# Storing the fp8 copy of an adjacency chunk one chunk later in the written order (20 slots behind its load instead of 10)

## The chip, the cores and the metric

The kernel runs on one core of a Trainium2 chip. A core has four engines that compute, each with its own queue of instructions: TensorE (PE, matrix products), VectorE (DVE), ScalarE (ACT) and GpSimd (POOL). A fifth, SyncE (SP), issues DMAs. DMAs are issued here from the queues of SyncE, of GpSimd and, at the start, of ScalarE. The metric is the time of one execution on the device in microseconds (us); of several runs the median is taken.

## The reference, cut to what matters

Sixteen graphs of 1024 nodes with 128 features go through four layers, each `x = layernorm(x + layer(x, adj))`. `adj` is a 0/1 matrix in float32, one for each graph.

```
layer 0: masked attention: softmax over the neighbours of relu(q) relu(k)^T, times relu(v)
layer 1: h[n] = max over m of relu(x[n] (W1 - W2) + x[m] W2 + b) * adj[n, m]
layer 2: MLP((1 + eps) x + adj^T x), masked by node
layer 3: adj_d = dilate(adj)            # a row-by-row removal of edges, each row seeing earlier removals
         three rounds of batchnorm(relu(sage(h, adj_d))), then a linear layer of the three results
```

Two parts of this set the kernel's shape. Layer 1 is a maximum over neighbours, not a product, and the removal of edges in layer 3 is serial over the 1024 rows. The removal depends on the adjacency alone, so it can run beside layers 0 to 2.

## The kernel before, in words

Layers 0 to 2 and the removal of edges share one long stage, the function `layers_012`; layer 3 follows.

**The slots.** Layer 1 takes 12 neighbours at a time (`PS`, L44). For each such group a table over the subsets of its two halves of six is built, and each node looks up the best neighbour in its subset by matrix products. A graph has 86 groups (`NP`, L47), and one group of one graph is a *slot*: 16 x 86 = 1376 slots, in the loop at L932, each written out by `slot` (L861). In a slot, PE multiplies the transposed adjacency by a table of signs (`count`, L812) to find the subset of every node, ACT turns the result into a one-hot matrix (L813), PE looks up (L843), and DVE takes the maximum (L908). Between these steps a planner in the kernel (`advance`, `dilate_on`) puts in the other layers' work and the removal.

**The chunks.** The transposed adjacency arrives in chunks of 120 rows (`CH`, ten groups of 12), nine for a graph, the ninth of 64 rows. `load_columns(at)` (L753) does two things for chunk number `at`, counted through all graphs, 0 to 143. It writes the *store* of chunk `at - 1` (L758), a DMA on SyncE's queue that copies the fp8 chunk from the buffer AT to the DRAM tensor `adj8`, which layer 3 reads in place of the float32 original (`load_near`, L993). Then it writes the *load* of chunk `at` (L764), a DMA on GpSimd's queue that reads float32 and writes fp8 into AT. AT has four buffers (L761), so the load of chunk `at` writes where chunk `at - 4` was, and needs that one's store and its matrix products to be done. The first two calls are at L916; then `slot` calls it at every tenth group (L873), two chunks ahead of the one in use.

**What sets the order.** Inside the block at L930, PE, ACT, DVE and POOL take their instructions in the order in which the kernel writes them. SyncE isn't among them: the order of its DMAs is made by the scheduler that builds the program. Each queue works from the front, so a DMA that waits for its input holds those behind it.

**What shares SyncE's queue.** The removal of edges goes over blocks of 32 rows. Per block it has `above` and V (L555, L556), the exchange of `hit` through DRAM (L686, L689), the results `removed` from the buffer `gone` (L615, two buffers, made at L613), `removed_T` (L622), and its reading back into `gone_T` (L517). Beside these are the loads of X (L747) and the stores of the layers' results (L466). After the slots come `near` (L995) and the weights of layer 3 (L118).

The store and the load, as written before:

```
nc.sync.dma_start(out=adj8[before][k * CH:k * CH + rows], in_=AT[at - 1][:rows])
...
nc.gpsimd.dma_start(out=t[:rows], in_=adjT[b, c * CH:c * CH + rows])
```

Of the kernel before, what the change touches and what calls it, by code (L numbers as in the profile page):

```python
# [39 lines left out]
B, N, D, H2 = 16, 1024, 128, 256  # L40
P = 128
T = N // P
GS = 6
PS = 2 * GS  # L44
PC = 10
CH = PC * PS
# [28 lines left out]
def tile_graph_layers(ctx: ExitStack, tc, a, out):  # L75
    nc = tc.nc
# [95 lines left out]
    for b in range(B):  # L172
        q, g = divmod(b, G)
        nc.gpsimd.dma_start(out=half_rows[g * R:(g + 1) * R, :, q],
                            in_=a["nodemask"][b].rearrange("(k r) -> r k", r=R))
# [21 lines left out]
    adj8 = [dram.tile([N, N], F8, name=f"adj8_{b}") for b in range(B)]  # L197
# [44 lines left out]
    def layers_012():  # L242
# [133 lines left out]
        def attend(b):  # L376
            for t in range(T):
                yield ask("PE", 0.01, after=("e", b, t))
                if t == 0:
                    y = w4.tile([P, T, D], F32, name="y0", tag="xT")  # L380
                e, total = exps.pop((b, t))
                eT = w4.tile([P, T, P], F32, name="eT")
                for h in range(2):
                    yield ask("PE", 0.44, take=True, same=(h == 0))
                    p = shared("pe")
                    for c in range(4):
                        nc.tensor.transpose(p[:, c * P:(c + 1) * P],  # L387
                                            e[:, (4 * h + c) * P:(4 * h + c + 1) * P], ident)
                    yield ask("A", 0.59, give=True, same=True)
                    nc.scalar.copy(eT[:, 4 * h:4 * h + 4, :].rearrange("p c i -> p (c i)"), p)  # L390
                happened["back", b, t] = now
                for h in range(4):
                    yield ask("PE", 0.45, take=(h == 0), same=(h > 0))
                    if h == 0:
                        pav = shared("pav")[:, :D]
                    for c in range(2 * h, 2 * h + 2):
                        nc.tensor.matmul(pav, eT[:, c, :], values[b][:, c, :], start=(c == 0), stop=(c == T - 1))  # L397
                yield ask("V", 0.4, give=True)
                share = small.tile([P, 1], F32, name="share")
                nc.vector.reciprocal(share, total)  # L400
                nc.vector.scalar_tensor_tensor(y[:, t, :], pav, share, X[b][:, t, :], op0=ALU.mult, op1=ALU.add)
            yield from norm(X[b], y)
            happened["X1", b] = now
# [66 lines left out]
        def tables_of(b):  # L470

            if b:
                yield ask("V", 0, urgent=True, after=("tables", b - 1))
            for g0 in range(0, NP, TG):
                n_g = 2 * min(TG, NP - g0)
                yield ask("V", 0.01, same=True, urgent=True, after=("q", b))
                made.append((b, g0))
                yield ask("V", 0.1, same=True, urgent=True, after=("used", *made[-3]) if len(made) > 2 else None)
                qg = qs[b].rearrange("o (g s) -> o g s", s=GS)
                subs[b, g0] = w2.tile([P, TG, P], F32, name="sub", bufs=2)  # L480
                sub = subs[b, g0].rearrange("o t (a s) -> o (t a) s", a=2)
                nc.vector.memset(sub[:, :n_g, 0:1], LOWEST)
                for k in range(GS):
                    n = 1 << k
                    yield ask("V", 0.06 + n * n_g / 960, same=(n < 8), urgent=True)
                    nc.vector.tensor_max(sub[:, :n_g, n:2 * n], sub[:, :n_g, 0:n],  # L486
                                         qg[:, 2 * g0:2 * g0 + n_g, k:k + 1].to_broadcast([P, n_g, n]))
                happened["sub", b, g0] = now
            happened["tables", b] = now
# [255 lines left out]
        def load_x(b):  # L745
            X[b] = apool.tile([P, T, D], F32, name="X", bufs=3)
            nc.sync.dma_start(out=X[b], in_=x[b].rearrange("(t p) d -> p t d", p=P))  # L747
# [4 lines left out]

        def load_columns(at):  # L753
            b, c = divmod(at, T + 1)
            if at:
                before, k = divmod(at - 1, T + 1)
                rows = min(CH, N - k * CH)
                nc.sync.dma_start(out=adj8[before][k * CH:k * CH + rows], in_=AT[at - 1][:rows])  # L758
            if b < B:
                rows = min(CH, N - c * CH)  # L760
                t = AT[at] = apool.tile([CH, N], F8, name="AT", bufs=4)  # L761
                if rows < CH:
                    nc.gpsimd.memset(t, 0.0)
                nc.gpsimd.dma_start(out=t[:rows], in_=adjT[b, c * CH:c * CH + rows])  # L764

        An, AT, subs, qs, ps, values, exps, bests, hots, tables = ({} for _ in range(10))
# [8 lines left out]
        def start(stream, first=False):  # L775
            pending[stream] = [next(stream, None), -9]
            streams.insert(0 if first else len(streams), stream)
# [52 lines left out]
        def low_part(s):  # L830
            pt, high = tables[s]
            nc.tensor.matmul(pt, less, high, start=False, stop=True, skip_group_check=True)  # L832
            low = w2.tile([P, 2 * P], F32R, name="low", bufs=2)
            nc.scalar.copy(low, pt)  # L834
            tables[s] = high, low

        def look_up(s, h, pg):

            at = s % 2
            for k, part in enumerate(tables[s - at]):  # L840
                for a in range(2):
                    rows = slice(64 * a, 64 * a + 64)
                    nc.tensor.matmul(pg[:, a], part[rows, at * P:(at + 1) * P], hots[s][rows, halves[h]],  # L843
                                     start=(k == 0), stop=(k == 1))
# [9 lines left out]
        def dilate_on():  # L854
            nonlocal due, wants_bank
            if due <= now and not (wants_bank and taken >= 2 and given.get(taken - 2, 1e9) > now):
                after, cost, wants_bank = next(dilate, (B * NP, 0, False))
                due += after
                room["V"] -= cost

        def slot(s, last):  # L861

            nonlocal now
            now = s
            b, g = divmod(s, NP)
            if s >= 0 and g == 0:
                bests[b] = bests[b - 1] if b else w4.tile([P, 2, N], F32, name="best")
                if b + 1 < B:
                    start(tables_of(b + 1), True)
                    load_x(b + 1)  # L870
                    start(attend(b + 1))
                    start(scores(b + 1))
            if s >= 0 and g % PC == 0 and b * (T + 1) + g // PC + 2 <= B * (T + 1):  # L873
                load_columns(b * (T + 1) + g // PC + 2)
            for h in range(2):
                now = s + 0.5 * h
                for e in ROOM:
                    room[e] = min(room[e] + ROOM[e] / 2, ROOM[e] / (2 if e in ("PE", "V") else 1))
                if s >= 0:
                    pg = psum.tile([P, 2, 512], F32, tag="wide", name="pg", bufs=2)  # L880
                    look_up(s, h, pg)
                early = s >= 0 and due < now
                if early:
                    dilate_on()
                advance(("PE",))
                advance(("A", "V", "Pool"))
                if s >= 0 and not early:
                    dilate_on()
                if h == 0 and s % 2 and s + 1 < last:
                    low_part(s + 1)  # L890
                if s + 2 < last:
                    count(s + 2, h)
                    if h and s % 2 == 0:
                        table(s + 2)
                if s >= 0:
                    own = bests[b][:, :, halves[h]]
                    if g == 0:
                        if b:
                            if h:
                                merge(b - 1, h)  # L900
                            total(b - 1, h)
                        nc.vector.tensor_copy(own, pg)
                        if b and h:
                            start(rest(b - 1))
                    else:
                        if g == NP - 1 and h:
                            merge(b, 0)
                        nc.vector.tensor_max(own, own, pg)  # L908
            if s >= 0:
                hots.pop(s)  # L910
# [19 lines left out]
        with tc.manual_schedule(engines={mybir.EngineType.PE, mybir.EngineType.Activation, mybir.EngineType.DVE,  # L930
                                         mybir.EngineType.Pool}):
            for s in range(-2, B * NP):  # L932
                slot(s, B * NP)
# [437 lines left out]
```

## Time and profile before

| what | value |
|---|---|
| median of three runs | 6206.11 us |
| the three runs | 6195.82, 6206.11, 6211.7 us |
| the profiled execution | 6199.75 us, span 6198.0 us |
| granted TensorE clock, mean | 0.962 |
| stage of the slots | about 90 to 5085 us of the span |
| layer 3 after it | 5085 to 6198 us |
| chunk stores at L758 | 144, on SyncE's queue, first at 28.2 us, last at 5023.5 us |
| chunk loads at L764 | 144, on GpSimd's queue, first at 19.8 us, last at 5020.3 us |
| a load from issue to landing | 2.9 us least, 3.9 median, 29.7 most |

The *span* runs from the first to the last instruction of the profiled execution. *Busy* is the time in which an engine computes; issuing a DMA isn't counted as busy, so SyncE has no busy time, and what it does is read from its waits and its timeline. In a view of waits, a row has the engine that waited and the line of the instruction, then what it waited for, then the total in us, the number of waits and the longest one. SPq is SyncE's queue. In a timeline, a row has the start in us, the duration, the engine, the line and the operation; rows of the same kind that follow each other are merged, with their number at the end (x2), and the duration then runs from the first start to the last end. What stands in brackets is idle time of the engine before the instruction and what ended it. *Landing* is the moment at which a DMA's data have arrived.

### The profile page before, as it was taken

Reading aid. Unit: us, or ns where it says so; the run is one execution under the profiler, and the core shown is the slowest. Engines: PE = TensorE matmul, PEld = TensorE weight load, DVE = VectorE, ACT = ScalarE, POOL = GpSimd, SP = SyncE. Lnnn points to the kernel's source line nnn. Section 1 sums busy time; section 2 is a strip of 40 time slices with the busy share of each in tenths; the row PEclk is TensorE's granted clock in tenths of the full one; section 3 lists DMA queues with packets and bytes.
Section 4 is the critical chain, followed back from the end, with each engine's and each line's share of the span. In section 5 each row is a group of like instructions: output and inputs, shape, how many; then the busy total and the mean of one; then the engine's idle time right before and its main releaser. Section 6 shows DMA issues by size and latency. Waiting matters only on the chain.

```text
span 6198.0 us, 93287 instructions
## 1 busy us (share of the span) xinstructions
PE 5582.7 (90%) x30144; PEld 3046.0 (49%) x30250; DVE 4870.0 (79%) x7484; ACT 3988.2 (64%) x7362; POOL 3613.1 (58%) x11879
## 2 busy tenths in 40 slices
PE   5989899989898989999989798989999878999998
PEld 4545454545454545454545454545444435555654
DVE  3888788888888888889888788888889875555455
ACT  3767676767676767677767576767666554344855
POOL 2676666667666767677777757667677651110114
PEclk8999999989999999999999899999999989999999
DMA  5021213121212212122121211212121014554645
GB/s 42 11 33 25 40 22 42 22 40 24 40 24 31 32 32 32 32 32 38 26 43 22 39 24 31 31 31 33 31 33 28 19 41 124 159 144 133 214 163 191
DMA packets 496976, 334.28 MB, mean 54 GB/s; under 512 B 303338, under 2 KB 448228, under 8 KB 492388
## 3 DMA queue, kind: packets, MB, share of 16 engines
q1 hardware_dynamic: 405504, 260.29, 14.5%
q0 software_dynamic: 89008, 67.42, 12.6%
q8 instruction: 237, 3.88, 0.3%
q14 instruction: 255, 2.09, 0.1%
q10 hardware_dynamic: 1972, 0.59, 0.1%
HBM read 362.38 MB, written 133.96 MB: 80 GB/s over the span
## 4 chain that ended last, share of the span: by engine, by line
PE 31%; DVE 10%; ACT 4%; POOL 3%; issue 2%; DMA 1%; SPq 0%; DVEq 0%; POOLq 0%; ACTq 0%
PE pg L843 7%; PE pagg L1071 5%; DVE best L908 5%; PE pm L812 3%; PE po L1101 2%; PE po L1095 1%; PE pa L439 1%; PE pav L397 1%; PE pp L300 1%; ACT hot L813 1%; PE pdeg L1026 1%; DVE near L1014 1%; PE psc L349 1%; PE prank L599 1%; PE pe L387 1%
## 5 line engine op out<-in xcount | busy, mean ns | idle before, releaser
L908 DVE TENSOR_TENSOR best<-best,pg 128x1024 f32<-128x1024 f32 x2720 | 3259.3, 1214 | 512.6 <-PE pg L843 501.7
L813 ACT ACTIVATE hot<-pm,one_less 128x512 fp32r<-128x512 f32 x2752 | 1887.4, 689 | 780.5 <-PE pm L812 773.2
L843 PE MATMUL pg<-hot,high 64*128 64x512 f32 x5504 | 1407.3, 508 | 258.9 <-DVE best L908 220.8
L843 PE MATMUL pg<-hot,low 64*128 64x512 f32 x5504 | 1115.5, 402 | 0.0
L812 PE MATMUL pm<-AT,lit 120*128 120x512 fp8e4 x2752 | 1085.9, 395 | 4.5 <-ACT low L834 3.5
L843 PEld LDWEIGHTS pg<-hot,high 64*128 64x128 f32 x5504 | 523.5, 187 | 1014.6 <-DVE best L908 492.8
L669 POOL TENSOR_SCALAR sc<-low_counts,half_mask,rest 16x1 f32<-16x1 f32 x992 | 354.4, 357 | 393.9 <-DVE rest L655 283.2
L843 PEld LDWEIGHTS pg<-hot,low 64*128 64x128 f32 x5504 | 537.9, 192 | 0.0
L812 PEld LDWEIGHTS <-lit 120*128 120x128 fp8e4 x2752 | 270.3, 98 | 389.8 <-issue 313.5
L674 POOL TENSOR_SCALAR sc<-sc 16x1 f32<-16x1 f32 x992 | 393.1, 396 | 105.1
L834 ACT CAST low<-pt 128x256 fp32r<-128x256 f32 x688 | 256.0, 372 | 263.3 <-PE pt L832 261.9
L671 POOL TENSOR_SCALAR sc<-sc 16x1 f32<-16x1 f32 x992 | 324.5, 327 | 107.6
L1116 POOL TENSOR_TENSOR length<-length,mhalf 128x8 f32<-128x8 f32 x48 | 78.9, 1644 | 489.2 <-DVE length L1115 489.2
L676 POOL TENSOR_SCALAR hit<-V,sc 16x31 bf16<-16x31 bf16 (+30 forms) x992 | 362.4, 365 | 0.0
L677 POOL TENSOR_SCALAR last_rank<-V,sc 16x31 f32<-16x31 bf16 (+30 forms) x992 | 342.9, 346 | 0.0
L832 PE MATMUL pt<-high,less 128*128 128x256 f32 x688 | 279.2, 406 | 67.6 <-ACT high L827 61.5
L824 PE MATMUL pt<-ident,sub 128*128 128x128 f32 x1376 | 277.5, 283 | 51.8 <-ACT hot L813 50.0
L486 DVE TENSOR_TENSOR sub<-sub,q 128x24 f32<-128x24 f32 (+11 forms) x768 | 304.0, 397 | 24.8 <-ACT q L304 10.4
L397 PE MATMUL pav<-v,eT 128*128 128x128 f32 x2048 | 301.5, 292 | 2.0 <-ACT eT L390 2.0
L397 PEld LDWEIGHTS pav<-v,eT 128*128 128x128 f32 x2048 | 255.4, 196 | 73.3 <-issue 55.7
L670 POOL TENSOR_SCALAR sc<-sc 16x1 f32<-16x1 f32 x992 | 237.0, 239 | 86.5
L349 PE MATMUL psc<-kT,qT 128*128 128x256 f32 x1024 | 276.3, 388 | 9.9 <-issue 9.9
(270 smaller groups left out, 9662.9 us busy)
## 6 DMA issues: line engine op xcount, KB each, us to landing
removed<-gone SPq DMA_DIRECT2D x128, 256.0 KB
An<-in_adj_dram POOLq DMA_DIRECT2D x16, 1024.0 KB, 16.0
E<-in_adj_dram POOLq DMA_DIRECT2D x128, 128.0 KB, 6.6
gone_all<-removed POOLq DMA_DIRECT2D x64, 256.0 KB, 10.2
near<-adj SPq DMA_DIRECT2D x16, 1024.0 KB
kept<-near SPq DMA_DIRECT2D x16, 1024.0 KB
share<-share SPq DMA_DIRECT2D x32, 512.0 KB
hidden<-r SPq DMA_DIRECT2D x32, 512.0 KB
```

Source lines behind the costliest of these rows:

```text
L349: nc.tensor.matmul(psc[:, 256 * i:256 * (i + 1)], qT[:, t * P:(t + 1) * P], kT[:, s.start + 256 * i:s.start + 256 * (i + 1)], start=False, ...
L397: nc.tensor.matmul(pav, eT[:, c, :], values[b][:, c, :], start=(c == 0), stop=(c == T - 1))
L669: gp.tensor_scalar(half, mine, half_mask[:, m], rest[:, n:n + 1], op0=ALU.mult, op1=ALU.add)
L671: gp.tensor_scalar(sf, half, 5.5, sf, op0=ALU.is_gt, op1=ALU.mult)
L674: gp.tensor_scalar(to, at, sf, none, op0=ALU.subtract, op1=ALU.subtract)
L676: gp.tensor_scalar(hit[:, n, n + 1:], V[:, n, n + 1:], at, None, op0=ALU.is_equal)
L677: gp.tensor_scalar(last[:, n + 1:], V[:, n, n + 1:], to, None, op0=ALU.is_le)
L812: nc.tensor.matmul(pm, lit[:, r, :], AT[b * (T + 1) + c][:, halves[h]], start=True, stop=True)
L813: nc.scalar.activation(hots[s][:, halves[h]], pm, AF.Relu, bias=one_less)
L843: nc.tensor.matmul(pg[:, a], part[rows, at * P:(at + 1) * P], hots[s][rows, halves[h]], start=(k == 0), stop=(k == 1))
L908: nc.vector.tensor_max(own, own, pg)
L1071: nc.tensor.matmul(pa[:, s], piece[:, t, :], m[c][:, s], start=(i == 0), stop=(i == 15))
```

## The change

`load_columns(at)` stores chunk `at - 2` instead of `at - 1`, so the store of a chunk is written 20 slots after its load was written instead of 10. The guard of the call in `slot` goes, so that there is one more call in the last graph, which writes the last store and no load.

```
         def load_columns(at):
             b, c = divmod(at, T + 1)
-            if at:
-                before, k = divmod(at - 1, T + 1)
+            if at > 1:
+                before, k = divmod(at - 2, T + 1)
                 rows = min(CH, N - k * CH)
-                nc.sync.dma_start(out=adj8[before][k * CH:k * CH + rows], in_=AT[at - 1][:rows])
+                nc.sync.dma_start(out=adj8[before][k * CH:k * CH + rows], in_=AT[at - 2][:rows])
             if b < B:
 ...
-            if s >= 0 and g % PC == 0 and b * (T + 1) + g // PC + 2 <= B * (T + 1):
+            if s >= 0 and g % PC == 0:
                 load_columns(b * (T + 1) + g // PC + 2)
```

## The prediction

> **What bounds the kernel now.** I read the first page first: busy shares, slices, and the chain of work that ended last.
>
> ```profile
> span 6198.0 us, 93287 instructions
> PE 5582.7 (90%) x30144; PEld 3046.0 (49%) x30250; DVE 4870.0 (79%) x7484; ACT 3988.2 (64%) x7362; POOL 3613.1 (58%) x11879
> PE 31%; DVE 10%; ACT 4%; POOL 3%; issue 2%; DMA 1%; SPq 0%; DVEq 0%; POOLq 0%; ACTq 0%
> ```
>
> PE is busy 90% of the span, and the named pieces of the chain are mostly its matmuls, then VectorE's maxima. DMAs are 1% of the chain and SyncE's queue 0%. A change to stores on SyncE's queue can therefore move the end only where an engine waits for something that is queued behind those stores. So the next view was what SyncE's queue waits for, in the stretch of the slots (90 to 5085 us):
>
> ```profile
> SPq L758 <- DMA AT<-in_adjT_dram: 2815.7, 135, 54.8
> SPq L686 <- POOL hit L678: 463.6, 24, 29.7
> SPq L615 <- DVE gone L613: 372.7, 47, 19.4
> SPq L555 <- DVE Vp L552: 256.9, 24, 80.8
> ```
>
> L758 is the store that the change is about, and it is by far the longest wait of this queue: 2815.7 us in 135 waits, 20.9 us each, for the load of its own chunk. That is odd for a store written one chunk (10 slots) after its load. The loads are issued from 19.8 to 5020.3 us, 144 of them, so a chunk is (5020.3 - 19.8) / 143 = 35.0 us, while a load lands 3.9 us (median) after its issue. If the store stood in the queue where the source puts it, SyncE would find the chunk long landed. The timelines of GpSimd (loads) and of SyncE (stores) between 1500 and 1700 us show why it doesn't; columns are start, duration, engine, line:
>
> ```profile
> 1510.96 0.62 POOL L764 DMA_DIRECT2D AT<-in_adjT_dram  x1 [0.36 <-PE pg L843]
> 1555.81 0.66 POOL L764 DMA_DIRECT2D AT<-in_adjT_dram  x1 [0.28 <-issue]
> 1588.50 0.66 POOL L764 DMA_DIRECT2D AT<-in_adjT_dram  x1 [0.29 <-POOL AT L763]
> 1641.98 0.71 POOL L764 DMA_DIRECT2D AT<-in_adjT_dram  x1 [0.33 <-PE pt L824]
> ```
>
> ```profile
> 1514.74 45.22 SPq L758 DMA_DIRECT2D adj<-AT  x2
> 1560.01 0.38 SPq L615 DMA_DIRECT2D removed<-gone  x1
> 1560.49 0.39 SPq L622 DMA_DIRECT2D removed_T<-last_T  x1
> 1591.52 0.45 SPq L758 DMA_DIRECT2D adj<-AT  x1
> 1592.06 0.54 SPq L615 DMA_DIRECT2D removed<-gone  x1
> ...
> 1645.85 0.35 SPq L758 DMA_DIRECT2D adj<-AT  x1
> ```
>
> Store less load: 1514.74 - 1510.96 = 3.8 us, 1591.52 - 1588.50 = 3.0 us, 1645.85 - 1641.98 = 3.9 us; the row of two ends at 1559.96, 4.2 us after the load at 1555.81. From the start times of all 144 pairs the median is 3.9 us, and only the first three are over 8. The store leaves when its own chunk lands, some 31 us earlier than "10 slots behind" would say. SyncE isn't among the engines that are held to the written order (L930 names PE, ACT, DVE and Pool). For SyncE the scheduler puts a DMA where its input comes free in the scheduler's own reckoning, and for this store that is the landing of its load. The place in the source ranks a DMA only among those free at the same moment.
>
> **What the Trainium skill says.** "DMA: Bandwidth & Descriptors", section "Anatomy of one DMA — SWDGE (gpsimd) path": DMA engines don't wait on semaphores; the wait is taken by the issuing sequencer before dispatch. The trace agrees: the 2815.7 us stand on SyncE's queue, and at 1591.52 a store held until its landing is followed at once by L615 and L622. The same section prices a transfer at 2.0 us and bytes / 436e3; for a chunk's 120 x 1024 x 4 B that is an estimate of 3.1 us, the trace has 3.9 from issue to landing. Section "Rules for kernel authors" of that page: issue a DMA early and wait on its semaphore late. Here the wait comes early, which matters for the first rival.
>
> **The change part by part.**
>
> 1. The store names chunk at-2 instead of at-1. The load and its place among GpSimd's instructions don't change. In the changed program as it is built, each of the five engines has the same instructions in the same order, on the same buffers and addresses, with the same waits; only running numbers in names differ. The reason is the reading above: a store that goes when its load lands, and not when it is written, isn't moved by being written later. Cost: 0 of 144 stores moved x any price = 0 us. The 2815.7 us of waits stay, and so does what is queued behind them (L615, L622, L686 and the X loads).
>
> 2. The guard of the call is dropped, so one more call comes at g = 80 of the last graph. It loads nothing (b = 16) and stores chunk 143. Calls 2 to 145 give 144 stores, as calls 1 to 144 did. 0 instructions, 0 us.
>
> 3. The four AT buffers. A load into a buffer must wait for the store that read it. By start times, the load of chunk i+4 comes at least 100.7 us after store i, and stays so. 0 us. Nothing hides this cost; there is no added work to hide.
>
> 4. The tail. The loads of `near` (L995) and of the third layer's weights (L118) follow the last store on SyncE's queue; the last is issued at 5023.5 us, the first weight at 5087.3. Unmoved: 0 us.
>
> Sum: the profiled execution took 6199.75 us (6198.0 of span and 1.75 around it); 6199.75 + 0 = 6199.75. It lies 6.36 below the median of the three runs, 6206.11, within their 6195.82 to 6211.7. The forecast for a median is 6206.11 + 0, so 6206. About 0.3% (18.6 us) is what a measurement of this kernel can tell from no change.
>
> **Rivals.**
>
> *Noise alone* isn't a mechanism, but has a size: the three runs spread over 15.9 us, 0.26%. Two medians of the same program can differ by a good part of that; over 18.6 us I give 1 in 100 on each side.
>
> *Rival one, faster: the stores do move on the chip, and SyncE is free for what is behind them.* What it could give is bounded by what engines now wait for from SyncE's DMAs, in the view of all waits over the slots:
>
> ```profile
> DVE gone L613 <- DMA removed<-gone: 80.6, 9, 18.0
> PE ptr L290 <- DMA X<-in_x_dram: 28.7, 4, 20.3
> DVE hit_T L703 <- DMA hit_p<-hit: 23.6, 2, 14.4
> PEld ptr L290 <- DMA X<-in_x_dram: 20.7, 1, 20.7
> ```
>
> DVE waits 80.6 us because `gone` has two buffers and their stores to `removed` (L615) stand behind a held chunk store, as at 1592.06. All four lines together are 153.6 us, the most, if each lay on the path: 6206.1 - 153.6 = 6052.5. The two DVE lines alone are 104.2 us: 6102. For it speaks that these waits are real and that a store written 20 slots (70 us) behind its load would find it landed. Against it, decisively, stands that the queue's order isn't the written one: before, 10 written slots already became 3.9 us. Chance 0.02.
>
> *Rival two, slower: the stores come late and hold the AT buffers.* Written places taken at their word put store i 70.0 us after its load instead of 3.9, so 66.1 later. Of the 100.7 us until the load of i+4, 34.6 remain, less about 3.9 for the store to land (taken like a load of the chunk): 30.7 us. It decides from a store held over 30.7 us more, and then GpSimd stops at L764 with the dilation's serial steps (L669 to L679) queued behind it, and DVE and PE behind those. The longest hold of SyncE by a single wait is 80.8 us (L555 on Vp), so 80.8 - 30.7 = 50.1 us for one such event: 6256. One such hold in 24 is that long (24 waits are 256.9 us together), so one event. Against it: the buffer's release is the landing of the store, and the store isn't moved. Chance 0.01.
>
> *That the change doesn't do what it says* is here the forecast itself. Chance 0.97.
>
> **How the numbers follow.** The 0.97 give 0.95 within 0.3%, 0.01 below and 0.01 above by noise. Faster: 0.01 + 0.02 = 0.03. Slower: 0.01 + 0.01 = 0.02. Same: 0.95. The range is that of noise, since the rivals together hold 0.03: the runs' own spread, 15.9 us, to each side of the median is 6190 to 6222. Neither 6102 nor 6256 needs to be in it.
>
> **What would show it.** In the profile of the changed kernel: 144 stores at L758 each 3 to 4 us after their load at L764, not 35 or 70; about 2800 us of waits of SyncE's queue at L758; DVE's waits at L613 for `removed` near 80 us; 93287 instructions, PE busy near 5583 us; a span within 18.6 us of 6198. A wait at L758 that falls below, say, 1000 us would mean that the stores did move, and rival one. GpSimd stopping at L764 for a DMA from AT would be rival two. The prediction is wrong if the order on the chip isn't the built one, or if something outside the instruction streams (where code or data lies in memory) moves the time by over 0.3%; neither shows in a profile of before.

## The result, and the profile after

| | before | after |
|---|---|---|
| median of twelve runs each | 6199.57 us | 6205.93 us |
| lowest to highest | 6186.83 to 6211.7 us | 6188.37 to 6218.97 us |
| span of the profiled execution | 6198.0 us | 6196.8 us |

The ratio of after to before is 1.0007, with a 95% interval of 0.9995 to 1.002: no difference that can be measured. (The ratios in this document are the recorded ones, formed over the runs; they need not be the quotients of the two medians.) The first page of the profile after has the same count of instructions and the same shares:

```profile
span 6196.8 us, 93287 instructions
PE 5584.1 (90%) x30144; PEld 3047.8 (49%) x30250; DVE 4872.2 (79%) x7484; ACT 3988.4 (64%) x7362; POOL 3611.7 (58%) x11879
```

PE moved by 1.4 us, DVE by 2.2, GpSimd by 1.4. What SyncE's queue waits for, in the stretch of the slots:

```profile
SPq L758 <- DMA AT<-in_adjT_dram: 2810.5, 135, 54.8
SPq L686 <- POOL hit L678: 462.6, 24, 28.9
SPq L615 <- DVE gone L613: 382.2, 51, 18.0
SPq L555 <- DVE Vp L552: 259.0, 24, 79.9
```

The store still waits 135 times for its own load, 2810.5 us against 2815.7. DVE's wait for the stores of `removed` is there too:

```profile
DVE gone L613 <- DMA removed<-gone: 83.4, 11, 18.0
```

The timelines of GpSimd and of SyncE show nearly the same distance between a load and its store as before, 3.96 us here (1511.02 - 1507.06) against 3.8:

```profile
1507.06 0.62 POOL L764 DMA_DIRECT2D AT<-in_adjT_dram  x1 [0.36 <-PE pg L843]
1551.91 0.65 POOL L764 DMA_DIRECT2D AT<-in_adjT_dram  x1 [0.29 <-issue]
```

```profile
1511.02 45.05 SPq L758 DMA_DIRECT2D adj<-AT  x2
1556.13 0.38 SPq L615 DMA_DIRECT2D removed<-gone  x1
1556.60 0.39 SPq L622 DMA_DIRECT2D removed_T<-last_T  x1
```

Over all 144 pairs the median distance is 3.9 us, as before. A store 20 slots behind its load would be 70 us away. And by operation and tile names, the 1226 DMAs of SyncE's queue follow each other in the same order in the two traces, as do the instructions of the other four engines. The text of the kernel changed, the order of the queue did not.

### The profile page after: what moved, and what is told of

It reads as the page before. It is cut to its first block, busy times and chain, and to the rows that moved or that the text cites. A ratio compares the mean times of both kernels' runs of the same rounds, so it can differ in the third digit from the quotient of the medians.

```text
span 6196.8 us, 93287 instructions
## 1 busy us (share of the span) xinstructions
PE 5584.1 (90%) x30144; PEld 3047.8 (49%) x30250; DVE 4872.2 (79%) x7484; ACT 3988.4 (64%) x7362; POOL 3611.7 (58%) x11879
## 4 chain that ended last, share of the span: by engine, by line
PE 30%; DVE 9%; ACT 4%; POOL 4%; issue 2%; DMA 2%; SPq 0%; DVEq 0%; POOLq 0%; ACTq 0%
PE pg L843 7%; PE pagg L1071 5%; DVE best L908 4%; PE pm L812 2%; PE po L1101 2%; PE po L1095 1%; PE pa L439 1%; PE pav L397 1%; ACT hot L813 1%; PE pp L300 1%; PE pdeg L1026 1%; DVE near L1014 1%; PE psc L349 1%; PE prank L599 1%; DVE sub L486 1%
```

## The experiments

Two questions were left. Does the written place really count for nothing? And what would the move have been worth if it had reached the queue? The prediction's first rival said 104 us for that, and its second feared for the AT buffers.

**The store written in the same call as its load (0 slots behind), nothing else changed.**

```
             if b < B:
                 ...
                 nc.gpsimd.dma_start(out=t[:rows], in_=adjT[b, c * CH:c * CH + rows])
+                nc.sync.dma_start(out=adj8[b][c * CH:c * CH + rows], in_=t[:rows])
```

(The store at the head of `load_columns` goes.)

> The store written in the same call as its load, 0 slots behind it, nothing pinned. If the written place only ranks the store among those free at the same moment: the same instructions in the same order as before on every queue, store less load 3.9 us, DVE's 80 us at L613 and 2800 us of SyncE's waits at the store kept, time within 0.3% of before. If the written place counts on the chip in any other way: away from before by over 0.3%, slower by the direction in which 10 slots gained.

Measured: 6206.11 us against 6203.82 for before, ratio 1.0004 (0.9994 to 1.0014). Store less load is 3.9 us (median of 144). In the waits over the slots, the load of the chunk holds SyncE 135 times as before, and DVE still waits for `removed`:

```profile
SPq L761 <- DMA AT<-in_adjT_dram: 2817.2, 135, 55.0
```

```profile
DVE gone L613 <- DMA removed<-gone: 83.5, 10, 18.0
PE ptr L290 <- DMA X<-in_x_dram: 27.1, 4, 19.0
```

The DMAs of SyncE's queue stand in the order of before in this trace as well. So 0, 10 and 20 slots give one order on the chip.

**The store held to its written place: 10, 20 and 30 slots.** The kernel has a helper, `behind` (L237), that makes an instruction come after another one for the scheduler alone, with no semaphore. With it the store can't go into the queue ahead of the work that is written before it:

```
+                last = nc.cur_bb.bb.instructions[-1]
+                n = len(nc.cur_bb.bb.instructions)
                 nc.sync.dma_start(out=adj8[before][k * CH:k * CH + rows], in_=AT[at - 1][:rows])
+                if slots:
+                    behind(last, n)
```

(`slots` is false for the two calls ahead of the loop. With `at - 2` this is the change made effective; with `at - 3`, and one more call after the last chunk, it is 30 slots. The order of PE, ACT, DVE and GpSimd stays as before. In the traces of 10 and 20 slots the other 1082 DMAs of SyncE keep their order among themselves, so only the stores moved; with 30 slots three of the others change places.)

> The chunk store is held, for the scheduler alone and without a new semaphore, behind the instruction that the kernel wrote just before it, so that it stands in SyncE's queue where before.py writes it, 10 slots behind its load. Both theories: store less load about 35 us, SyncE's waits at the store fall from 2815 us to under 300. Theory 1 (what was held behind the stores lies off the path): time within 0.3% of before, DVE's 80 us at L613 gone or not. Theory 2 (it lies on the path): 100 us less, about 0.984 of before, with DVE's wait for removed under 30 us.

> As the run with 10 slots, but with the changed kernel's place, 20 slots behind the load: the change made effective. Both theories: store less load about 70 us, SyncE's waits at the store under 300 us. Theory 1: within 0.3% of before and of the run with 10 slots. Theory 2: about 0.984 of before. If the AT buffers came late (the slower rival), GpSimd would wait at the chunk load for a DMA, 50 us or more.

> The store at 30 slots behind its load, pinned. With four AT buffers the load of chunk i+4 then comes only one chunk, about 35 us, after the store of chunk i. Both theories on what is held behind the stores say the same as for 20 slots. The slower rival decides here if anywhere: where SyncE is held for longer than about 31 us, GpSimd waits at the chunk load, up to 50 us each time; if that happens often, slower than before by over 0.3%. If SyncE is not held that long, no difference from 20 slots.

| store held to its place | median | ratio to before, 95% interval | store less load, median |
|---|---|---|---|
| before, in these rounds | 6200.94 us | | |
| 10 slots | 6097.85 us | 0.9834 (0.9819 to 0.985) | 28.0 us |
| 20 slots | 6091.23 us | 0.9833 (0.9817 to 0.9848) | 63.2 us |
| 30 slots | 6090.1 us | 0.9832 (0.9812 to 0.9852) | 93.9 us |

Theory 2 holds: what stood behind the stores was on the path. By the medians 103 us came back with 10 slots and 110 and 111 with 20 and 30; the ratios of the three are alike. The distances are a little short of the expected 35 and 70 us, and with 10 slots 26 of the 144 stores still leave within 8 us of their load. In the view of SyncE's waits with 10 slots, the store no longer heads the list:

```profile
SPq L615 <- DVE gone L613: 1832.7, 119, 55.1
SPq L686 <- POOL hit L678: 710.2, 24, 75.2
...
SPq L760 <- DMA AT<-in_adjT_dram: 78.5, 21, 11.4
```

SyncE waits about as long as before: over the slots, all its waits together are 4619 us, against 4655. But it now waits mostly with `removed` at the front, which goes out as soon as DVE has made `gone`, and in the view of all waits no engine waits for a chunk store that comes late. A hold of 78.5 us at the store is left. In the view of all waits, of those for a DMA from SyncE over the slots one is left that counts:

```profile
DVE hit_T L703 <- DMA hit_p<-hit: 26.5, 3, 16.3
```

The lines of L613 for `removed` (80.6 us before) and of L290 for X (28.7 and 20.7) are gone.

**Which of the two waits.** Before, the `removed` stores that DVE waited for stood behind the stores of the last two chunks of a graph (k = 7 and 8), and the two late X loads (3548.4 and 3869.6 us) behind that of k = 2. For the first of these loads, TensorE's two rows in the views (PE, its products, and PEld, the loading of its weights) are one and the same wait, as the timeline of before shows:

```profile
3561.55 1.11 PE L290 MATMUL ptr<-ident,X 128*128 128x128 f32 x4 [20.32 <-DMA X<-in_x_dram]
3561.55 0.71 PEld L290 LDWEIGHTS ptr<-ident,X 128*128 128x128 f32 x4 [20.75 <-DMA X<-in_x_dram]
```

So TensorE's waits for X are 28.7 us, this one and one of 8.0 us for the second load above all, and not the 49 us to which the two rows add up. The expectation of the second run below counts the one wait twice. The pin at 10 slots was given to part of the stores:

```
-                if slots:
+                if slots and k in (7, 8):
                     behind(last, n)
```

(and in the other run `k in (2, 3)`)

> Only the stores of the last two chunks of each graph (k = 7 and 8) are pinned to their written place, 10 slots behind the load; the other seven stay where the scheduler puts them. In the profile of before the removed stores that DVE waits for (80.6 us at L613) stand behind these two. If the 104 us of the full pin are those waits: DVE's wait at L613 for removed under 20 us, PE's waits for X (20 us twice) unchanged, time about 0.988 of before (70 us less). If the X loads carry the gain instead: 0.997 or more.

> Only the stores k = 2 and 3 of each graph are pinned. Behind k = 2 stood the two X loads that PE waited for, about 20 us each, and behind k = 3 some removed stores that nobody waited for. If the waits add up: PE's waits for X gone (49 us in the view, 40 us as two events), DVE's 80 us at L613 kept, time about 0.994 of before (30 to 45 us less). If only the removed stores count: within 0.3%.

Measured, against 6211.2 us for before in these rounds: with k = 7 and 8, 6131.68 us, ratio 0.9873 (0.9856 to 0.989); with k = 2 and 3, 6172.98 us, ratio 0.9942 (0.9924 to 0.996). The waits for DMAs, first with 7 and 8 pinned:

```profile
PE ptr L290 <- DMA X<-in_x_dram: 28.3, 3, 19.5
...
PEld ptr L290 <- DMA X<-in_x_dram: 19.9, 1, 19.9
...
DVE gone L613 <- DMA removed<-gone: 0.5, 1, 0.5
```

and with 2 and 3 pinned:

```profile
DVE gone L613 <- DMA removed<-gone: 84.8, 10, 18.1
...
PE ptr L290 <- DMA X<-in_x_dram: 0.5, 1, 0.5
```

Each pin takes away its own wait and leaves the other's. With DVE's wait of 80.6 us went 79.5 us of time (6211.2 - 6131.68), with PE's waits of 28.7 us went 38.2 us. The sum, 117.7, is somewhat above the 103 of the full pin; the intervals, some 10 us to each side, don't tell these apart.

These gains are not the waits alone, since the granted TensorE clock rose too: its mean over the runs is 0.968 in each of the three full pins against 0.962 for before in the same rounds, and 0.965 and 0.964 in the two partial ones against 0.960. In 62 runs whose queue order is that of before, a run takes about 3.6 us less for each 0.001 of clock. By that, some 20 us of a full pin's gain and 15 to 17 us of a partial one's go with the clock; at an equal clock the partial pins would give about 62 and 21 us and the full ones 86 to 88. This is an estimate from the means of those runs. Whether the shorter waits raised the clock is open.

Removed stores stood behind k = 2 and 3 as well, but in the trace of before DVE waited for none of those, and with 2 and 3 pinned its wait at L613 is unchanged.

**The whole queue in written order.** SyncE is added to the engines at L930, so all its DMAs of the slots stand where they are written. That moves more than the stores: some 290 of the 1082 others change places too.

```
             with tc.manual_schedule(engines={mybir.EngineType.PE, mybir.EngineType.Activation, mybir.EngineType.DVE,
-                                             mybir.EngineType.Pool}):
+                                             mybir.EngineType.Pool, mybir.EngineType.SP}):
```

> SyncE joins the engines that are held to the written order through the slots, so all its DMAs stand where the kernel writes them; stores 10 slots behind. If holding of any kind on SyncE is what costs: at least the gain of the pin, 0.983, perhaps 20 us more for the waits on hit_p, 0.980. If the written order puts DMAs that wait long ahead of urgent ones: slower than the pin, with new waits for X, hit_p or V.

> As the run before it, with the changed kernel's place, 20 slots behind the load. If the change of place is worth nothing once the store isn't held: within 0.3% of the run with 10 slots in full written order, by time and by waits. If the second chunk of distance counts: faster by over 0.3%. If it holds the AT buffers: GpSimd waits at the chunk load for a DMA, and slower.

Measured: 10 slots 6092.63 us, ratio 0.9813 (0.9795 to 0.9832); 20 slots 6086.09 us, ratio 0.9803 (0.9787 to 0.9819). SyncE's waits at the store with 10 slots:

```profile
SPq L758 <- DMA AT<-in_adjT_dram: 148.2, 25, 31.8
```

With 20 slots the only wait left there is 24.2 us. Here the change is real: it takes 124 us of waits from the queue. But by time the two agree within their intervals, and the waits of engines for DMAs from SyncE are alike in both. The hoped-for gain on hit_p didn't come: DVE's wait for it is 24.1 and 26.8 us. Nor did new waits for X or V come, with which the expectation had reckoned. The run with 20 slots has the lowest ratio of all, 125 us below before, and also the highest mean clock, 0.970; against the pin the intervals overlap.

**The AT buffers made to bind.** The pin at 30 slots with three buffers instead of four:

```
-                t = AT[at] = apool.tile([CH, N], F8, name="AT", bufs=4)
+                t = AT[at] = apool.tile([CH, N], F8, name="AT", bufs=3)
```

> The store pinned 30 slots behind its load, and three AT buffers instead of four, so that the load of chunk i+3 is written right behind the store of chunk i and must wait for it: the slower rival made true. If the buffers decide: in the run with four buffers the load of i+4 came 4.6 us (least) and 44 us (median) after the store of i; one chunk less (35 us) leaves a median of about 9 and many below zero, so GpSimd waits at the chunk load in some 40 of 144 loads, 10 to 30 us each, 400 to 1000 us in all, with the serial removal behind it: 1.0 or more of before, the pin's gain lost. If GpSimd has that much slack: waits at the load, and still 0.983.

Measured: 6093.26 us against 6203.82, ratio 0.9825 (0.9811 to 0.9838). The gain is all there: the first branch of the expectation, 1.0 or more, missed, and the second, waits at the load and still 0.983, came. GpSimd does wait at the load, most in these rows of its waits:

```profile
POOL sc L669 <- DVE rest L655: 232.5, 29, 15.5
POOL num L707 <- DVE counts L530: 213.8, 27, 21.9
...
POOL AT L768 <- PE pm L816: 73.2, 34, 9.9
POOL AT L768 <- PE pg L847: 59.6, 24, 11.7
...
POOL AT L768 <- DMA adj<-AT: 26.5, 9, 8.1
POOL AT L767 <- DMA adj<-AT: 19.4, 5, 8.9
```

All rows at AT together are 227 us; with 30 slots and four buffers they were 49 us. That is 178 us more, less than the 400 expected, in pieces of at most 11.7 us. The view puts most of them down to PE. But by the times of the semaphores in the trace, 32 of the waits of over 1 us, 148 us together, ended within 0.75 us of the landing of the store of the chunk that was in that buffer; nine more, 46 us, ended otherwise. With four buffers, GpSimd's first two waits were longer:

```profile
POOL num L707 <- DVE counts L530: 315.0, 30, 23.1
POOL sc L669 <- DVE rest L655: 287.8, 30, 15.5
```

With three they are less by 101.2 and 55.3 us, 156.5 of the 178. GpSimd stood idle there, waiting for DVE some 30 times in each row, and a delay at the chunk load was taken out of that idle time. That both amounts are the same idle time is argued from the sums; the runs show that the wait came and the time did not.

## Why the prediction was right

*The reading of the queue.* It rested on one comparison: a store written 10 slots behind its load, in a kernel with 35.0 us to 10 slots, left 3.9 us after it. So the queue wasn't in written order, and a new written place had nothing to act on. After the change the distance is 3.9 us again, and with the store written 0 slots behind too. That it is the scheduler which makes the order was argued there; the pins bear it out, since they speak to the scheduler alone, add no semaphore, and the stores moved.

*The parts.* Each of them was put at 0 us, and the sum of 0 us stands: the ratio is 1.0007 with 1 inside its interval, and 6205.93 us lies in the range of noise that was given. That it falls within 0.1 us of the forecast 6206 is luck: the kernel before, in its four sets of runs, had medians from 6199.57 to 6211.2 us. The marks that were named came: a median of 3.9 us from load to store (the first three are over 8, as before), 2810.5 us of waits at L758, 83.4 us at L613 for `removed`, 93287 instructions, a span 1.2 us from that of before.

*Rival one* was a sound account of something that this change doesn't do. Its 6102 us is close to the 6097.85 of the store pinned at 10 slots, but its makeup was wrong. It took DVE's two lines (80.6 and 23.6); what went away was the 80.6 and PE's waits for X, 28.7 us, while the 23.6 for hit_p stayed. That its 6102 lies so near is therefore partly luck. Its bound of 153.6 us counts one wait of TensorE twice, in the rows of PE and PEld; without that it is about 133. The two waits that went make 109.3 us, and 103 showed, a part of it with the clock. That DMAs are 1% of the chain was no measure of what the stores held up: 1% of the span is 62 us.

The Trainium skill's rule, in "DMA: Bandwidth & Descriptors", section "Rules for kernel authors", is to issue a DMA early and wait on it late, so that its fixed setup cost overlaps with other work. The pins fit the second half, waiting late, but for another reason than the one named there: the store's early wait hurt nobody who needed the store, only those behind it in the queue (80.6 us of DVE's waits at L613, gone with the pin).

*Rival two* was priced wrong. It took a stop of GpSimd at the chunk load to be a delay of the end, 50 us for one hold. With 178 us more of GpSimd's waits there, the time didn't move. Nor did holds of SyncE bring such waits at 20 slots: one hold grew to 103.5 us (80.8 had been taken), and GpSimd's waits at AT were 42 us, as against 41 before. Its 30.7 us of slack wasn't the limit either: with 30 slots and four buffers a load came within 4.6 us of the store before it in the same buffer, with no loss.

## What to carry to other kernels

Before judging an edit that moves a DMA in the source, compare the start of that DMA with the start of what it depends on, in the trace: if the distance isn't the written one, the order is made elsewhere, and the edit changes nothing. A long wait of a queue costs nothing by itself; look at who stands behind it, and at which engine waits for those. Here the waits of engines for such DMAs, 80.6 us on DVE and 28.7 us on PE, went away once the harmless store no longer stood in front, and 103 us came back, some 20 of them with a higher clock. And before adding up rows of a view of waits, see in the timeline whether two rows are one wait.

## What the runs showed that had not been expected

A queue's total wait says little. With the store pinned at 10 slots, SyncE still waits 1832.7 us at L615 alone, and yet the kernel is 103 us faster: what changed is what stood at the front. And GpSimd, which carries the serial removal of edges, took 178 us of added waits at the chunk loads with no change of time (0.9825 against 0.9832 with a fourth buffer, intervals overlapping).

Left open: how much of the gain is the waits themselves and how much the higher clock, and whether the clock rose because of them; whether the 26 us that DVE still waits for hit_p can be had. No run moved that exchange alone. A third buffer for `gone`, which might take away DVE's wait at L613 with no store moved, wasn't tried.
